# The last quarter of the last unit: activation and product in two halves, written to the buffer of an x

## The chip, the cores and the metric

The kernel runs on one core of a Trainium2 chip. The metric is the device time of one execution in microseconds (us). The engines are named as in the profile: PE (TensorE, products of matrices), PEld (its weight loads), DVE (VectorE), ACT (ScalarE), POOL (GpSimd), and SP (SyncE), which only issues transfers. ACT and POOL issue transfers too. Each engine works through its own queue in order; semaphores tie the queues together.

## What is computed

An input `x` of 16 batches, 256 rows and 256 columns, in float32, goes through two mixtures of experts, each added to its input. In the first, one expert of eight is chosen for each batch, with biases and a hidden width of 512. In the second, two experts of eight are chosen and weighted, and a shared expert is added for every batch, with a hidden width of 1024.

```python
# first layer, for each batch, with its expert's weights
x = x + (silu(x @ wu.T + bu) * (x @ wg.T + bg)) @ wd.T + bd
# second layer: two chosen experts, weighted, and the shared one
mlp = lambda g, u, d: (gelu(x @ g) * (x @ u)) @ d
x = x + w1 * mlp(*expert1) + w2 * mlp(*expert2) + mlp(*shared)
```

## The kernel before

Everything is kept transposed, features on the partitions and the 256 rows of a batch along the free dimension. The work is cut into units. A `Pair` is one expert with two batches; a `Single` has one batch. A pair's products are done in Strassen's way: the two batches and the two halves of a matrix make a 2 by 2 block product, which takes seven products (steps) in place of eight and some sums of blocks.

A pair of the second layer goes through four *quarters*, each a quarter of the hidden width. A quarter has seven *up* steps (`up`, L541): step by step they fill PSUM banks named X, Y and Q. ACT copies each X bank to SBUF (`copy`, L522), and DVE combines such a copy with a Y or Q bank (`combine`, L526) into one of four blocks of the tile `c`: C11, C21, C12, C22. The blocks are complete after different steps: C11 after step 1, C22 after step 4, C21 after step 5, C12 after step 6. C11 and C21 belong to the first batch of the pair, C12 and C22 to the second. When all are there, `act` applies the activation to the gate half of `c` (ACT, L577) and multiplies it by the other half (DVE, L580) into a tile of the ring `bt`; `act_sums` then adds up the blocks that the next product needs (`sums_b`, L472 to L474).

After the four quarters follow seven *down* steps (`down`, L597), each with eight matmul pieces over the four quarters' `bt` tiles, into banks A, B and Y. After a step whose bank is complete for the first time, `early` moves the bank to a small tile `dz` (ACT, L619; in the last unit DVE, L612, which adds what already stands in the output). When the second part is there, `late` adds it and writes a block of the result `ys` (L630). The first down step reads only block C11 of each quarter's activations, the second only C21, and the others read sums too.

The units overlap. The down steps of one unit are put among the up steps of the next. The order is made when the kernel is built: `Line` keeps a clock in units of PE work, `main` emits a piece and moves the clock, and `later` puts a piece at a due time, so that the order in each engine's queue is that of the due times. Buffers come from rings. Some rings, `bt` with seven tiles among them, are *held*: a tile goes back by `give`. If none is free when a piece is due, `when_free` keeps the piece until a `give` emits it. The ring `xt`, with two tiles as wide as those of `bt`, is not held and is used in turn; it holds the `x` of a unit and of the next.

The last two units are pairs of the shared expert, `shared[-2]` and `shared[-1]`. For the last one, the activation of its fourth quarter is due when all seven `bt` tiles are out: four belong to `shared[-2]`, three to its own earlier quarters. It is therefore emitted by the first `give` at the end of `shared[-2]`'s seventh down step, after that step's late sum on DVE:

```python
elif k == 6:
    late(C12, "Q", -1)
    give("d", self)
    for j in range(self.kp):
        give("bt", (self, j))
```

The results of a unit are added to the output in memory by accumulating transfers on POOL's queue (`send`, L451), one for each batch; for `shared[-2]` they are issued at once after its last down step. Each is given the rows of its batch by an index that is loaded at run time, and waits for the one before. The last unit does without: it loads what stands in the output into `z` beforehand (L515), adds it in `early`, and stores plainly, block by block, the first batch on SP's queue and the second on ACT's (L633). The first of these stores on each queue waits until POOL's transfers have landed; SP's second store also waits until SP's first has landed. After its last store each engine branches to a common end block (L1096 in the profile), where SP waits for all transfers and the engines meet.

Which experts fall in pairs is known only at run time; the program holds an arm for each case, and every arm ends with the same two shared units.

Of the kernel before, what the change touches and what calls it, by code (L numbers as in the profile page):

```python
# [10 lines left out]
AF = mybir.ActivationFunctionType  # L11
ALU = mybir.AluOpType
# [3 lines left out]
B, S, D, E = 16, 256, 256, 8  # L16
# [39 lines left out]
UP, SINGLE_UP = 2, 8  # L56
# [3 lines left out]
def kernel(  # L60
# [10 lines left out]
    nc = tc.nc  # L71
# [40 lines left out]
    def take(tag, *shape, of=None):  # L112

        i = turns[tag].pop(0)
        if tag not in HELD:
            turns[tag].append(i)
        else:
            assert (tag, of) not in turns
            turns[tag, of] = i
        t = rings[tag][i]  # L120
        n = 1
        for d in shape:
            n *= d
        t = t[:, :n]
        if len(shape) == 1:
            return t
        names = "abcd"[: len(shape)]
        return t.rearrange(
            f"p ({' '.join(names)}) -> p {' '.join(names)}", **dict(zip(names, shape))
        )  # L130

    def when_free(tag, f):

        if turns[tag] and not turns["later", tag]:
            f()
        else:
            turns["later", tag].append(f)

    def give(tag, of):
        turns[tag].append(turns.pop((tag, of)))  # L140
        if turns["later", tag]:
            turns["later", tag].pop(0)()

    def bank(tag):
        return take(tag, N2)
# [312 lines left out]
    class Pair(Unit):  # L458
# [114 lines left out]
        def act(self, j):  # L573
# [6 lines left out]
            nc.vector.tensor_tensor(t[:, 0:4, :], u, v, ALU.mult)  # L580
            self.acts.append(t)

        def act_sums(self, j):
            t = self.acts[j]
            self.sums_b(t, t[:, 2, :])

        def down(self, k):

            tag, a, b = STEPS[k]
            if k == 0:  # L590
                self.ys = take("ys", KD, 2, S, of=self)
            if OPENS[k]:
                self.banks[tag] = bank({"X": "A", "Q": "B", "Y": "Y"}[tag])
            src = self.d[:, A_AT[a]] if a in A_AT else self.ds[:, S_AT[a]]
            d = self.banks[tag][:, :S]
            for j in range(self.kp):
                nc.tensor.matmul(  # L597
                    d,
                    lhsT=src[:, j, :],
                    rhs=self.acts[j][:, B_AT[b], :],  # L600
                    start=OPENS[k] and j == 0,
                    stop=j == self.kp - 1,
                    skip_group_check=True,
                )

            def early(block):
                c, t = block % 2, block // 2
                e = take("dz", S, of=(self, block))
                self.copies[block] = e
                src = self.banks["X"][:, :S]  # L610
                if self.last:
                    nc.vector.tensor_tensor(e, self.z[:, c, t, :], src, ALU.add)  # L612
                elif not self.layer:
                    nc.vector.scalar_tensor_tensor(  # L614
                        e, src, self.bd[:, c : c + 1], self.xt[:, block, :], ALU.add, ALU.add
                    )
                else:
                    w = 1.0 if self.at is None else self.weight(t)
                    nc.scalar.activation(e, src, AF.Copy, scale=w)  # L619

            def late(block, tag, sign):
                c, t = block % 2, block // 2
                e, src = self.copies[block], self.banks[tag][:, :S]
                dst = self.ys[:, c, t, :]
                if self.layer and self.at is not None:
                    nc.vector.scalar_tensor_tensor(  # L626
                        dst, src, self.weight(t, sign), e, ALU.mult, ALU.add
                    )
                else:
                    nc.vector.tensor_tensor(dst, e, src, ALU.add if sign > 0 else ALU.subtract)  # L630
                if self.last:
                    queue = (nc.sync, nc.scalar)[t]
                    store = queue.dma_start(self.out[t][:, c, :], dst)  # L633
                    for other in self.stores[1 - t]:
                        tc.declare_no_dep(store.ins, other.ins, reason="another batch")
                    self.stores[t].append(store)
                give("dz", (self, block))

            if k == 0:
                early(C11)  # L640
            elif k == 1:
                late(C11, "Y", 1)
            elif k == 2:
                early(C12)
            elif k == 4:
                early(C22)
                early(C21)
                late(C22, "Q", -1)
            elif k == 5:
                late(C21, "Y", 1)  # L650
            elif k == 6:
                late(C12, "Q", -1)
                give("d", self)
                for j in range(self.kp):
                    give("bt", (self, j))
                if not self.layer:
                    give("bt", self)
                if not self.last:
                    self.done(self.ys)

        def run(self, line, among):

            self.start()
            for j in range(self.kp):
                line.quarter(self, j)
                for k in range(6):
                    line.main(UP, lambda j=j, k=k: self.up(j, k))

                line.later(2 * UP, lambda j=j: self.up(j, 6))
                if not self.layer:  # L670
                    line.later(UP + 1, lambda j=j: self.act0(j, 1))
                line.later(
                    3 * UP, lambda j=j: when_free("bt", lambda: self.act(j))
                )
                line.later(6 * UP, lambda j=j: self.act_sums(j))
                for f in among[j] if j < len(among) else ():
                    f()
            step = self.step or (6 if self.layer else 3)
            for k in range(7):
                line.later(self.first + step * k, lambda k=k: self.down(k))  # L680
# [262 lines left out]
    line = Line()  # L943
# [55 lines left out]
    def follow(units, behind=True):  # L999
# [3 lines left out]
        if known == start + Q_AHEAD - 1:  # L1003
            u, j = quarters[known]
            u.load_q(j, behind=behind)

    run(units[0])
    for k in arms(0):

# [10 lines left out]
        for a, p in zip(places[4:], pieces):  # L1020
            a.append(p)
        follow([*mid, *units[1], *tails[1]], behind=False)
        run([*mid, *units[1]])
        while line.routed < len(steps):
            line.route()
        for k in arms(1):
            left = ones[2 * k :]
            rest = [*tails[1], *left[:-1], *more_pairs[:k], *shared[1 - NB :]]
            turns["xs"], turns["d"] = [0, 1], [*turns["d"], 2]
            for u in rest:  # L1030
                among[u] = [[] for _ in range(u.kp)]
            if left:

                host = rest[len(left)]
                for j in range(host.kp):
                    among[host][j].append(partial(left[-1].piece, line, j, among=True))
                left[-1].po_bank, left[0].po_bank = "A", "B"
                shared[-NB].first = 24
            follow(rest)
            run(rest)  # L1040
            line.flush(1 << 30)
            line.send()
# [58 lines left out]
```

## Time and profile before

| | us |
|---|---|
| median of 3 runs | 1051.06 (1050.55 to 1051.47) |
| profiled execution | 1051.36 |
| its span | 1049.7 |
| PE busy | 1038.2 (99% of the span) |
| DVE busy | 777.0 (74%) |
| ACT busy | 371.3 (35%) |
| POOL busy | 446.7 (43%) |
| TensorE's granted clock | 0.999 |

The span is the time from the first to the last instruction of the profiled execution, which itself took 1.66 us more. Busy times overlap. Matmuls are pipelined and their ends are modelled, so that a matmul's reported duration overlaps the next. A time such as 1033.98 is counted from the start of the span. A wait for several semaphores is put down to the one that came last, which is not always the one that mattered.

### The profile page before, as it was taken

What the parts mean: (1) busy time and instruction counts of PE and PEld (TensorE: products, weight loads), DVE (VectorE), ACT (ScalarE), POOL (GpSimd) and SP (SyncE); (2) the same over time, 40 slices, a digit from 0 to 9 for tenths busy, and PEclk for the clock granted to TensorE, in tenths of its full rate; (3) what the DMA queues carried; (4) which work ended last, traced back from release to release, by engine and by line L of the source; (5) the groups of instructions that cost most, each with busy time, mean ns of one, the idle gap of its engine ahead of it and who ended that gap; (6) DMA issues with size and microseconds to landing.
All of it is one profiled execution on the core that took longest, in us unless ns stands there. A gap on an engine that the chain in (4) does not pass through costs nothing.

```text
span 1049.7 us, 14152 instructions
## 1 busy us (share of the span) xinstructions
PE 1038.2 (99%) x4750; PEld 900.3 (86%) x4750; DVE 777.0 (74%) x1207; ACT 371.3 (35%) x583; POOL 446.7 (43%) x492
## 2 busy tenths in 40 slices
PE   9999999999999999999999999999999999999998
PEld 6778888888888888888888888888888888888886
DVE  7789978878687877887777778777766236776764
ACT  2444353535333333333333333333333123333331
POOL 2946331221043765666476556645201245630000
PEclk9999999999999999999999999999999999999999
DMA  7636656656664355345335533543655445356522
GB/s 237 241 127 203 240 181 194 207 166 236 200 235 119 88 140 140 93 109 140 98 87 138 140 98 103 140 122 83 178 159 171 133 136 156 91 180 184 183 75 45
DMA packets 60974, 157.47 MB, mean 150 GB/s; under 512 B 7506, under 2 KB 27090, under 8 KB 56658
## 3 DMA queue, kind: packets, MB, share of 16 engines
q1 hardware_dynamic: 47618, 140.90, 40.3%
q0 software_dynamic: 12976, 15.21, 9.4%
q8 instruction: 42, 0.69, 0.3%
q14 instruction: 50, 0.41, 0.1%
q10 hardware_dynamic: 288, 0.26, 0.1%
HBM read 132.23 MB, written 24.12 MB: 149 GB/s over the span
## 4 chain that ended last, share of the span: by engine, by line
PE 89%; DVE 7%; issue 2%; ACT 1%; DMA 1%; SPq 0%; DVEq 0%; ACTq 0%
PE X L541 24%; PE Q L541 16%; PE Y L541 16%; PE A L597 12%; PE B L597 9%; PE Y L597 8%; DVE c L526 2%; PE X L692 2%; PE Q L692 1%; DVE bt L580 1%; PE A L722 1%; DVE bt L472 1%; DVE bt L473 1%; PE B L722 1%; ACT c L577 1%
## 5 line engine op out<-in xcount | busy, mean ns | idle before, releaser
L522 ACT ACTIVATE cp<-X 128x512 f32<-128x512 f32 x318 | 189.5, 596 | 519.2 <-PE X L541 518.6
L580 DVE TENSOR_TENSOR bt<-c 128x1024 f32<-128x1024 f32 x106 | 145.7, 1374 | 102.8 <-ACT c L577 93.0
L541 PE MATMUL Y<-xt,q 128*128 128x256 f32 x736 | 189.8, 380 | 1.1 <-DVE c L526 0.6
L541 PE MATMUL Q<-xt,s 128*128 128x256 f32 x736 | 189.5, 380 | 0.6 <-DVE c L526 0.6
L541 PE MATMUL X<-xt,s 128*128 128x256 f32 x736 | 189.5, 380 | 0.0
L526 DVE TENSOR_TENSOR c<-cp,Q 128x512 f32<-128x512 f32 x212 | 144.3, 681 | 37.4 <-ACT cp L522 32.9
L526 DVE TENSOR_TENSOR c<-cp,Y 128x512 f32<-128x512 f32 x212 | 144.1, 680 | 22.4 <-PE Y L541 22.0
L541 PEld LDWEIGHTS Y<-xt,q 128*128 128x128 f32 x736 | 138.9, 190 | 23.2 <-DVE c L526 3.9
L451 POOL DMA_DIRECT2D out_dram<-ys x46 | 49.0, 1065 | 255.7 <-DVE ys L626 103.2
L541 PEld LDWEIGHTS Q<-xt,s 128*128 128x128 f32 x736 | 139.3, 190 | 21.2 <-DVE c L526 2.5
L541 PEld LDWEIGHTS X<-xt,s 128*128 128x128 f32 x736 | 139.3, 190 | 20.5 <-ACT cp L522 1.4
L479 POOL TENSOR_TENSOR s<-q 128x256 f32<-128x256 f32 x78 | 72.1, 924 | 131.8 <-PE Q L541 66.2
L482 POOL TENSOR_TENSOR s<-s,q 128x256 f32<-128x256 f32 x78 | 62.5, 801 | 101.0 <-PE Q L541 101.0
L597 PE MATMUL A<-bt,ds 128*128 128x256 f32 x424 | 101.5, 379 | 1.4 <-DVE dz L614 1.4
L597 PE MATMUL B<-bt,ds 128*128 128x256 f32 x424 | 101.4, 379 | 0.0
L577 ACT ACTIVATE c<-c 128x1024 f32<-128x1024 f32 x92 | 96.7, 1052 | 12.9 <-DVE c L526 12.7
L472 DVE TENSOR_TENSOR bt<-bt 128x512 f32<-128x512 f32 x113 | 95.0, 840 | 0.7 <-DMA bt<-x_dram 0.6
L541 PE MATMUL X<-xt,q 128*128 128x256 f32 x368 | 94.4, 379 | 0.0
L597 PEld LDWEIGHTS A<-bt,ds 128*128 128x128 f32 x424 | 80.4, 190 | 13.0 <-POOL s L481 1.4
L597 PEld LDWEIGHTS B<-bt,ds 128*128 128x128 f32 x424 | 80.5, 190 | 11.2 <-ACT ys L737 0.3
L597 PE MATMUL Y<-bt,d 128*128 128x256 f32 x376 | 90.0, 379 | 0.0
L597 PEld LDWEIGHTS Y<-bt,d 128*128 128x128 f32 x376 | 71.4, 190 | 9.7
(163 smaller groups left out, 1157.1 us busy)
## 6 DMA issues: line engine op xcount, KB each, us to landing
q<-wq_dram SPq DMA_DIRECT2D x114, 512.0 KB, 3.7
d<-wd_dram SPq DMA_DIRECT2D x22, 1024.0 KB, 6.6
s<-qsums SPq DMA_DIRECT2D x28, 512.0 KB, 4.9
xt<-x1d SPq DMA_DIRECT2D x46, 256.0 KB, 4.3
out_dram<-ys POOLq DMA_DIRECT2D x46, 256.0 KB, 5.1
ds<-dsums SPq DMA_DIRECT2D x7, 1024.0 KB, 6.3
d<-wd_dram SPq DMA_DIRECT2D x7, 513.0 KB, 5.1
bt<-x_dram SPq DMA_DIRECT2D x14, 256.0 KB, 4.7
```

The costliest lines, as they stand in the source:

```text
L451: nc.gpsimd.dma_start(row(out), ys[:, :, t, :], accum_op=ALU.add)
L472: tt(t[:, 4:6, :], t[:, 0:3:2, :], t[:, 2:4, :], ALU.subtract)
L479: tt(s("S1"), a("A21"), a("A22"), ALU.add)
L482: tt(s("nS4"), s("S2"), a("A12"), ALU.subtract)
L522: nc.scalar.activation(t, self.banks["X", j], AF.Copy)
L526: nc.vector.tensor_tensor(self.c[j][:, block].rearrange("p m s -> p (m s)"), self.copies[n, j], self.banks[tag, j], op,)
L541: nc.tensor.matmul(self.banks[tag, j][:, bass.ts(m, S)], lhsT=self.q[j][:, m, A_AT[a], :] if a in A_AT else self.s[j][:, m, S_AT[a], :], r ...
L577: nc.scalar.activation(u, u, AF.Gelu_apprx_tanh)
L580: nc.vector.tensor_tensor(t[:, 0:4, :], u, v, ALU.mult)
L597: nc.tensor.matmul(d, lhsT=src[:, j, :], rhs=self.acts[j][:, B_AT[b], :], start=OPENS[k] and j == 0, stop=j == self.kp - 1, skip_group_che ...
L692: nc.tensor.matmul(dst[:, bass.ts(half, S)], lhsT=self.q[j][:, m, 2 * half + c, :], rhs=self.xt[:, c, :], start=(c == 0), stop=(c == KD - 1),)
L722: nc.tensor.matmul(self.po[:, bass.ts(c, S)], lhsT=self.d[:, 2 * c + half, j, :], rhs=self.acts[j][:, bass.ts(half, S)], start=(j == 0 and ...
```

## The change

In the last unit's fourth quarter, activation and product are done in two halves by batch. The first half (C11 and C21) is due one clock unit after the quarter's sixth up step is emitted, the second (C12 and C22) right after the seventh. The product is written to a tile of `xt`, so nothing has to be given back first; the pieces are no longer passed through `when_free`. The unit then gives back three `bt` tiles in place of four.

```diff
+        def act_half(self, j, half):
+
+            if half == 0:
+
+                self.acts.append(take("xt", 7, S))
+            t, k = self.acts[j], slice(2 * half, 2 * half + 2)
+            u, v = self.c[j][:, k, 0, :], self.c[j][:, k, 1, :]
+            nc.scalar.activation(u, u, AF.Gelu_apprx_tanh)
+            nc.vector.tensor_tensor(t[:, k, :], u, v, ALU.mult)
+
...
-                for j in range(self.kp):
+                for j in range(self.kp - self.last):
                     give("bt", (self, j))
...
-                line.later(
-                    3 * UP, lambda j=j: when_free("bt", lambda: self.act(j))
-                )
+                if self.last and j == self.kp - 1:
+
+                    line.later(1, lambda: self.act_half(j, 0))
+                    line.later(2 * UP, lambda: self.act_half(j, 1))
+                else:
+                    line.later(3 * UP, lambda j=j: when_free("bt", lambda: self.act(j)))
```

On each engine's queue in the arm that runs, this changes the end as follows. ACT has two activations of half the size in place of one, still ahead of its stores. DVE has this order:

```
before: sums of quarter 2 (L472 to L474), combine C12, late C21 and late C12 of
        shared[-2], product, sums of quarter 3, first early sum of the last unit
after:  sums of quarter 2, product half 0, combine C12, product half 1, late C21
        and late C12 of shared[-2], sums of quarter 3, first early sum
```

The orders on PE, POOL and SP stay as they were.

## The prediction

> **What bounds the kernel now.** I read the page first. Its busy row says that TensorE (PE) works without a break at full clock, so a gain can only come from a place where PE waits, or from the tail after its last product.
>
> ```profile
> span 1049.7 us, 14152 instructions
> ...
> PE 1038.2 (99%) x4750; PEld 900.3 (86%) x4750; DVE 777.0 (74%) x1207; ACT 371.3 (35%) x583; POOL 446.7 (43%) x492
> ```
>
> Next, PE's own waits over the whole span: the only one on a line that this change touches is 0.4 us behind the product of L580.
>
> ```profile
> PE A L597 <- DVE bt L580: 0.4, 1, 0.4
> ```
>
> The timeline shows where it stands: at 1033.98, in the last unit's first down step. Columns are start, duration, engine and line, with idle time in brackets.
>
> ```profile
> 1030.18 0.68 DVE L526 TENSOR_TENSOR c<-cp,Q 128x512 f32<-128x512 f32 x1
> ...
> 1030.78 0.42 DVE L630 TENSOR_TENSOR ys<-dz,Y 128x256 f32<-128x256 f32 x1
> 1030.95 1.06 ACT L577 ACTIVATE c<-c 128x1024 f32<-128x1024 f32 x1 [3.11 <-DVE c L526]
> 1031.49 1.08 POOL L451 DMA_DIRECT2D out_dram<-ys  x1 [31.09 <-DVE ys L630]
> ...
> 1032.37 0.42 DVE L630 TENSOR_TENSOR ys<-dz,B 128x256 f32<-128x256 f32 x1 [1.18 <-PE B L597]
> 1032.70 1.22 DVE L580 TENSOR_TENSOR bt<-c 128x1024 f32<-128x1024 f32 x1
> ...
> 1033.98 0.70 PE L597 MATMUL A<-bt,spare 128*128 128x256 f32 x2 [0.35 <-DVE bt L580]
> ...
> 1036.19 1.07 POOL L451 DMA_DIRECT2D out_dram<-ys  x1 [3.63 <-DVE dz L612]
> ```
>
> The activation was done at 1032.0, but its product stood on DVE behind the late sum of 1032.37, which waited for bank B. The bracket (0.35) understates the loss. In the chain of work that ended last, the step before ends at 1032.34; eight matmul pieces take 1.73 there, so the next step could begin at 1034.07. It begins at 1034.67:
>
> ```profile
> 1030.60 1.74 PE B L597 x8
> ...
> 1033.98 0.70 PE A L597 x2
> 1034.67 1.73 PE Y L597 x8
> ```
>
> PE loses **0.60 us**, and that is all the change can free.
>
> Last, the tail. PE's last sum is read at 1045.07; the final stores and the end of the program follow.
>
> ```profile
> 1040.94 3.19 SPq L633 DMA_DIRECT2D out_dram<-ys  x2
> ...
> 1042.74 3.13 ACTq L633 DMA_DIRECT2D out_dram<-ys  x2
> ```
>
> By the rows of L633, SP's two stores start at 1040.9 and 1043.8, ACT's at 1042.7 and 1045.5. SP's first could have gone at 1036.86, when its data was ready, but waits for the previous unit's two accumulating stores on POOL. Those are serial: the first starts at 1031.49 and lands after 4.1, at 1035.6, where POOL's last wait on L451 ends; the second starts at 1036.19 (the releaser that the timeline names, L612, only came last by chance), lands after 4.2, at 1040.4, and SP goes at 1040.94. SP's second store then waits for its own first (landed after 2.2, at 1043.16) and for data at 1043.77.
>
> [...] in the rows of the end block (first and last start):
>
> ```profile
> L1096 SPq EVENT_SEMAPHORE  x14: 17/28/28, 1046.9 to 1049.6; - x14
> ...
> L1096 SPq COMPARE_BRANCH  x2: 54/56/58, 1044.2 to 1044.7; - x2
> ...
> L1096 ACTq COMPARE_BRANCH  x2: 43/46/50, 1045.9 to 1046.3; - x2
> ...
> L1096 ACTq DRAIN  x2: 8/44/81, 1048.8 to 1049.1; - x2
> ```
>
> SP branches at 1044.7 and runs on at 1046.9, ACT at 1046.3 and 1048.8: 2.2 and 2.5 us that start only after each engine's last store. [...] the store at 994.1, with DVE busy throughout, lands after 4.3. What lengthens these stores in the trace is other traffic: the one at 957.9, beside 1.1 MB of loads, took 6.8.
>
> **The change, part by part.**
>
> *Moved.* The last activation and product leave the place behind the previous unit's last down step. [...] PE's, POOL's and SP's orders are unchanged, no DMA is added or moved past another, and ACT gains one instruction ahead of its final stores.
>
> *Price of the halves.* A product of 128x512 is not in the trace; the nearest row, L472 at 1033.96 (same size, two SBUF inputs), took 0.69. [...] Activation of 512: the copy of that size took 0.60[...]. I take 0.69 and 0.60; bounds 0.6 and 0.8. The pair costs DVE 0.16 more than one 1.22. The x buffer costs nothing: its last readers, the previous unit's up steps, ended four quarters earlier.
>
> *DVE worked out.* In this stretch an instruction that depends on nothing new starts 0.08 before its predecessor's reported end, a dependent one 0.03 after, and ACT 0.09 after DVE. C21's combine ends at 1028.74, so activation half 0 runs 1028.83 to 1029.43, hidden by the sums. Product half 0: 1030.18 (where C12 stood) to 1030.87. C12: 1030.79 to 1031.47. Activation half 1: 1031.56 to 1032.16. Product half 1: 1032.19 to 1032.88; DVE waits 0.7 for it. Queued behind it: late C21, 1032.80 to 1033.22 (before: 1030.78 to 1031.20); late C12 to 1033.55; the three sums to 1035.07; the first early sum 1035.00 to 1035.41 (before: to 1035.90).
>
> *PE.* It wants its first step's last pieces at 1033.64, when product half 0, the only one that step reads, has been there for 2.8 us: the stall of 0.60 goes. Next late would be the third step, which reuses bank A after the early sum: its first load moves from 1036.02 to 1035.42 against a sum ending at 1035.41, 0 to 0.05 lost. PE gains **0.57**; ACT's last store moves from 1045.53 to 1044.96.
>
> *The new wait.* Late C21 is the last input of POOL's first store and ends **2.0** later. Nothing hides that: POOL goes at 1033.49, lands 1037.6; the second goes 0.6 later, at 1038.2, and lands 1042.4; SP's first store 1042.94, landing 1045.16. SP's second, 0.53 after that landing, goes at 1045.7 instead of 1043.8. Its slack before was only 0.1: without the wait for data it would have gone at 1043.69.
>
> *The end.* SP's first wait of the end block came 3.1 after its last store, so now at 1048.8. Twelve waits at 0.06 and a drain follow: SP is done at about 1049.6 (before: 1048.4, itself waiting for ACT's last landing at 1047.96). Before, ACT was last, done at 1048.89; ACT would now be done at 1048.3. The end moves from 1048.89 to about 1049.6: **+0.7**. Bounds: if SP's first store lands with the bulk of its packets, 0.4 sooner, +0.3; if its second takes 3.9, as before, it lands at 1049.6 where SP wants it at 1049.1, +1.2.
>
> **Sum against its own time.** The profiled execution took 1051.36: span 1049.7 and 1.66 around it, 0.3 above the median of 1051.06. It would become 1052.1; the median, **1051.8**.
>
> **The rivals.**
> - *The stores have room* (late C21 is not held up, or POOL's stores land sooner). Then ACT still ends the kernel and all of PE's gain shows: 1051.06 - 0.57 = 1050.5. For it: PE leads the chain that ended last until 1045.05. Against: SP's slack of 0.1 against a delay of 2.0. Chance 0.13.
> - *Slower beyond doubt*: the shifted POOL stores take 5.8 each, as the one at 999.3 did, instead of 4.1 and 4.2. Each us passes through to SP: +3.3 on top of +0.7 gives 1055.1. It passes 0.2% once the two together are 1.4 us longer. For it: most such stores in the trace are that slow. Against: no weight loads remain at 1033 to 1042. Chance 0.06.
> - *It doesn't do what it says*: PE waits for both halves after all. Half 1 is there at 1032.88, still before 1033.64; same time as the forecast, 1051.8. Chance 0.02.
> - [...]
>
> The forecast itself has the remaining 0.79. The range runs from the full gain less some placement, 1050.0, to the forecast's upper bound plus placement, 1053.2. A measurement of this kernel can tell about 0.2%, 2.1 us, from no change; neither the forecast nor the first rival reaches that. Only the slow stores, or something that the trace does not show, do: slower 0.07, faster 0.03, no difference 0.90.
>
> **What would show it.** Right: no PE wait on the product in the last unit; two activations and two products of half size, the first product ahead of C12's combine; the late C21 sum about 2 us later, ending near 1033.2; POOL's last stores near 1033.5 and 1038.2; SP's second store near 1045.7, after ACT's last; the end block's first SP wait near 1048.8. Wrong: POOL's first store at 1031.5 as before, or SP's last store still ahead of ACT's (the gain then shows), or landings on POOL well above 4.2.

## The result and the profile after

The changed kernel takes **1053.84 us** (median of 9 runs, 1053.51 to 1055.40), the kernel before 1051.06 on the same chip (9 runs, 1049.94 to 1051.72). The ratio is 1.0031, 95% interval 1.0022 to 1.0040: slower, by 2.8 us. The forecast was 1051.8, in a range from 1050.0 to 1053.2, with a change too small to tell as the likeliest outcome. The kernel came out slower than all of that.

The profiled execution took 1053.84, with this span and these busy times:

```profile
span 1052.1 us, 14153 instructions
...
PE 1037.9 (99%) x4750; PEld 900.5 (86%) x4750; DVE 774.5 (74%) x1208; ACT 371.4 (35%) x584; POOL 446.4 (42%) x492
```

PE did the same work; what grew by 2.4 is the span. Up to the change everything lies 0.34 earlier than in the execution before (PE's B step ends at 1032.00 instead of 1032.34), so relative to that the end came 2.7 later. The line numbers have moved with the change: L590 and L591 are the new activation and product (`act_half`), L607 the down step (before L597), L640 the late sums (L630), L622 the early sum (L612), L643 the final stores (L633), L1109 the end block (L1096).

The timeline around the change (start, duration, engine, line; idle time in brackets):

```profile
1028.50 0.63 ACT L590 ACTIVATE c<-c 128x512 f32<-128x512 f32 x1 [0.99 <-DVE c L526]
...
1029.85 0.68 DVE L591 TENSOR_TENSOR xt<-c 128x512 f32<-128x512 f32 x1
...
1030.45 0.68 DVE L526 TENSOR_TENSOR c<-cp,Q 128x512 f32<-128x512 f32 x1
1031.17 0.63 ACT L590 ACTIVATE c<-c 128x512 f32<-128x512 f32 x1 [2.03 <-DVE c L526]
1031.83 0.69 DVE L591 TENSOR_TENSOR xt<-c 128x512 f32<-128x512 f32 x1 [0.70 <-ACT c L590]
...
1032.44 0.41 DVE L640 TENSOR_TENSOR ys<-dz,Y 128x256 f32<-128x256 f32 x1
...
1033.15 1.08 POOL L451 DMA_DIRECT2D out_dram<-ys  x1 [33.38 <-DVE ys L640]
...
1038.25 1.07 POOL L451 DMA_DIRECT2D out_dram<-ys  x1 [4.03 <-DMA out_dram<-ys]
```

The order on DVE is the one foretold: half 0, the combine of C12, 0.70 of waiting, half 1, and only then the late C21 sum, which ends at 1032.85 (before: 1031.20). POOL's store, which needs it, starts at 1033.15 instead of 1031.49. In the chain of work that ended last, PE no longer waits:

```profile
1030.28 1.73 PE B L607 x8
1032.00 1.73 PE A L607 x8
1033.73 1.73 PE Y L607 x8
...
1042.36 1.74 PE B L607 x8
1044.10 0.02 issue
1044.13 0.42 DVE ys L640
```

Each step begins where the one before ends. PE's last sum is read at 1044.13, 0.94 earlier than before, of which 0.34 is the head start: the change did free its **0.60**. Yet the kernel ends later. The rows of the final stores and of the end block (row: count: duration in ns, first and last start) say on which engine:

```profile
L643 ACTq DMA_DIRECT2D out_dram<-ys x2: 391/708/1026, 1043.1 to 1044.6; - x2
L643 SPq DMA_DIRECT2D out_dram<-ys x2: 338/358/377, 1043.4 to 1047.2; - x2
```

```profile
L1109 SPq EVENT_SEMAPHORE  x14: 17/28/28, 1050.5 to 1052.0; - x14
...
L1109 PEldq COMPARE_BRANCH  x2: 317/2584/4850, 1041.8 to 1042.2; - x2
...
L1109 ACTq DRAIN  x2: 8/44/81, 1048.5 to 1051.5; - x2
```

ACT's last store came 0.9 earlier than before (1044.6 for 1045.5), and its drain at 1048.5. SP's stores stand at 1043.4 and **1047.2**, where before they stood at 1040.9 and 1043.8; SP's first wait of the end block, 1046.9 before, is at 1050.5, and everyone waits for SP. The gap between SP's two stores, 2.9 before, is 3.7: the second waits for the first to land, and that took 3.6 instead of 2.2. What was on the DMA engines meanwhile (queue: packets, MB, share; then the stores of the window, with the time to landing; window 1042.6 to 1045.5):

```profile
q8 instruction: 2, 0.03, 8.1%
...
out_dram<-ys SPq DMA_DIRECT2D x1, 128.0 KB, 3.6
```

Queue q8 fetches instructions: two packets of 16 KB, from 1042.9 on, 0.7 after PE's second branch (1042.2) to the end block. In the execution before they came at 1043.8, when SP's first store (1040.9 to 1043.2) had landed, and at the same time as SP's second (1043.8). That one took 3.9 (before, same window):

```profile
q8 instruction: 2, 0.03, 7.6%
...
out_dram<-ys SPq DMA_DIRECT2D x1, 128.0 KB, 3.9
```

So the fetch met a store before as well, but the last on its queue, which no other store waits for.

### The profile page after: what moved, and what is told of

Its sections match the earlier page's. It is cut to its first block, busy times and chain, and to the rows that moved or that the text cites. A ratio compares the mean times of both kernels' runs of the same rounds, so it can differ in the third digit from the quotient of the medians.

```text
span 1052.1 us, 14153 instructions
## 1 busy us (share of the span) xinstructions
PE 1037.9 (99%) x4750; PEld 900.5 (86%) x4750; DVE 774.5 (74%) x1208; ACT 371.4 (35%) x584; POOL 446.4 (42%) x492
## 4 chain that ended last, share of the span: by engine, by line
PE 88%; DVE 5%; POOL 2%; issue 2%; DMA 1%; ACT 1%; SPq 0%; POOLq 0%; ACTq 0%; DVEq 0%
PE X L541 23%; PE Q L541 16%; PE Y L541 16%; PE A L607 12%; PE B L607 9%; PE Y L607 8%; DVE c L526 2%; PE Q L705 1%; PE X L705 1%; DVE bt L472 1%; POOL s L479 1%; PE B L735 1%; PE A L735 1%; DVE bt L580 1%; ACT c L577 1%
## 5 line engine op out<-in xcount | busy, mean ns | idle before, releaser
L607 PE MATMUL A<-bt,ds 128*128 128x256 f32 x420 | 100.6, 379 | 1.5 <-DVE dz L624 1.5
L607 PE MATMUL B<-bt,ds 128*128 128x256 f32 x420 | 100.5, 379 | 0.0
L607 PEld LDWEIGHTS A<-bt,ds 128*128 128x128 f32 x420 | 79.6, 190 | 13.0 <-POOL s L481 1.4
L607 PE MATMUL Y<-bt,d 128*128 128x256 f32 x376 | 90.0, 379 | 0.0
L607 PEld LDWEIGHTS B<-bt,ds 128*128 128x128 f32 x420 | 79.7, 190 | 11.1 <-ACT ys L750 0.3
L607 PEld LDWEIGHTS Y<-bt,d 128*128 128x128 f32 x376 | 71.4, 190 | 9.7
```

What stands on the lines that cost most here:

```text
L607: nc.tensor.matmul(d, lhsT=src[:, j, :], rhs=self.acts[j][:, B_AT[b], :], start=OPENS[k] and j == 0, stop=j == self.kp - 1, skip_group_che ...
```

## The experiments

My theory after the result had two parts. First, the late C21 sum behind the second half delays POOL's two stores and SP's two, as forecast. Second, this moves SP's first store into PE's instruction fetch, which holds up its last packets. The rivals: the halves themselves or the new buffer cost the time, by where instructions come to lie or by a wait that I had overlooked; or any later end of PE would save as much. Each ratio below is to the kernel before, run beside the experiment, with its 95% interval.

**The buffer alone.** Activation and product stay whole and stay where they were; only the tile is an `xt`.

```diff
+        def act_whole(self, j):
+            t = take("xt", 7, S)
+            u, v = self.c[j][:, :, 0, :], self.c[j][:, :, 1, :]
+            nc.scalar.activation(u, u, AF.Gelu_apprx_tanh)
+            nc.vector.tensor_tensor(t[:, 0:4, :], u, v, ALU.mult)
+            self.acts.append(t)
...
-                    line.later(1, lambda: self.act_half(j, 0))
-                    line.later(2 * UP, lambda: self.act_half(j, 1))
+                    line.later(3 * UP, lambda j=j: self.act_whole(j))
```

> The buffer alone: the last quarter's activation and product stay whole, but go to an x buffer and are due after the late C21 sum of the unit before (one activation, one product, no halves). Theory (the late C21 sum's place on DVE decides, through POOL's two serial stores and SP's two): the sum stays where it was before the change, so POOL's first late store starts within 0.3 us of its old place, SP's second store does not come after ACT's second, the product ends about 0.4 us ahead of PE's need, so PE's wait of 0.6 us is gone: 1050.5 us, against 1051.1 before and 1053.8 after. Rival (another buffer and other code places cost the time, whatever the order): about 1053.8.

Measured: 1050.47, ratio 0.9993 (0.9986 to 0.9999). Its timeline:

```profile
1030.82 0.41 DVE L647 TENSOR_TENSOR ys<-dz,Y 128x256 f32<-128x256 f32 x1
...
1032.09 1.22 DVE L597 TENSOR_TENSOR xt<-c 128x1024 f32<-128x1024 f32 x1 [0.85 <-ACT c L596]
```

The C21 sum (L647) is ahead of the product, both of SP's stores are early (1041.2 and 1043.4), and the new buffer costs nothing. It is the fastest version of all that ran, if only by 0.7 us.

**The whole product, early.** The same with due time `2 * UP`: no halves, but the product goes ahead of the late C21 sum.

> As the buffer alone, but the whole activation and product are due two clock units earlier, so that on DVE the product stands ahead of the late C21 sum: the delay without the halves. Theory (the sum's place decides): the sum waits for activation and product, some 2.4 us later than before the change, 0.4 later than with halves; PE's wait is gone all the same: 1053.5 to 1054.5 us. Rival (the halves themselves, with one more instruction each on ACT and DVE, cost the time): no halves here, so 1050.5 to 1051.1.

Measured: 1053.88, ratio 1.0027 (1.0016 to 1.0039), as slow as the change. Its timeline, and its row of the final stores:

```profile
1031.22 1.22 DVE L597 TENSOR_TENSOR xt<-c 128x1024 f32<-128x1024 f32 x1 [1.18 <-ACT c L596]
...
1032.36 0.41 DVE L647 TENSOR_TENSOR ys<-dz,Y 128x256 f32<-128x256 f32 x1
```

```profile
L650 SPq DMA_DIRECT2D out_dram<-ys x2: 338/358/378, 1042.7 to 1047.3; - x2
```

The halves aren't needed for the loss; the order on DVE is enough.

**The second half one clock unit later.** The change, with half 1 behind the late C21 sum.

```diff
-                    line.later(2 * UP, lambda: self.act_half(j, 1))
+                    line.later(2 * UP + 1, lambda: self.act_half(j, 1))
```

> The change, with its second half due one clock unit later, so that the late C21 sum stands ahead of the second product on DVE; both halves and the x buffer stay. Theory: the sum comes only 0.6 us later than before the change (behind the first product), SP's first store near 1041.5 in the time of the trace of before, its second near 1044.3, and ACT ends the kernel: 1050.6 us; if SP's first store already meets the transfers that slow it in the changed kernel, up to 1052.7. Rival (halves or code places): 1053.8.

Measured: 1051.08, ratio 1.0002 (0.9993 to 1.0010). The timeline:

```profile
1031.16 0.42 DVE L640 TENSOR_TENSOR ys<-dz,Y 128x256 f32<-128x256 f32 x1
...
1031.93 0.69 DVE L591 TENSOR_TENSOR xt<-c 128x512 f32<-128x512 f32 x1 [0.36 <-ACT c L590]
```

The C21 sum starts 1.3 earlier than with the change, SP's stores stand at 1041.4 and 1043.6, and the loss is gone. These three runs settle which part of the edit costs: putting half 1 ahead of that sum.

**The halves alone.** Halves in a `bt` tile, in the old place, through `when_free`.

```diff
+        def act_halves(self, j):
+            t = take("bt", 7, S, of=(self, j))
+            for half in range(2):
+                k = slice(2 * half, 2 * half + 2)
...
```

> The halves alone: activation and product in two halves by batch, but in a bt tile and in the old place, after the late C21 and C12 sums. Theory (PE's first down step needs only the first half, done about 0.2 us ahead of need; the sums stay in place): PE's wait is gone and the time is that of the buffer alone, 1050.5 us. Rival (one more instruction on ACT and DVE in every arm, or the halves, cost the time): about 1053.8.

Measured: 1051.47, ratio 1.0008 (0.9999 to 1.0016). That is 1.0 over what was expected, and no gain over the kernel before (1050.69 beside it), but far from 1053.8. PE has one wait there that the change has not, 0.2 behind the early sum for bank A. I can't tell this version from the kernel before, and why it isn't as fast as the buffer alone stays open.

**Block C21's final store on POOL's queue.** To take away SP's second wait, the store of C21 moves from SP to POOL, first in the change, then in the buffer alone.

```diff
...
-                    queue = (nc.sync, nc.scalar)[t]
-                    store = queue.dma_start(self.out[t][:, c, :], dst)
+                    q = 2 if block == C21 else t
+                    queue = (nc.sync, nc.scalar, nc.gpsimd)[q]
+                    store = queue.dma_start(self.out[q][:, c, :], dst)
...
```

> The change, with one store moved: block C21 of the last unit goes out on POOL's queue in place of SP's, so that it no longer waits for the landing of SP's first store. The late C21 sum and POOL's accumulating stores stay as late as in the changed kernel. Theory (the end hangs on SP's second store behind the landing of its first): SP is in the end block by about 1046.6 in the time of the changed trace, POOL's store starts near 1042.9 and lands by 1047.5, and ACT ends the kernel: 2.5 to 2.8 us less, about 1051.1. Rival (DVE's, PE's or the code's part in the change costs the time, SP's second store is only late and not the cause): about 1053.8.

> The buffer alone (whole activation and product in an x buffer, after the late C21 sum), and block C21's store on POOL's queue. Theory (in the buffer alone ACT's last store and its branch already end the kernel): no gain over the buffer alone, 1050.5 us. Rival (SP's second store still sets part of the end there): up to 0.5 us less, 1050.0.

Measured: 1052.58, ratio 1.0018 (1.0010 to 1.0026), and 1052.48, ratio 1.0016 (1.0010 to 1.0023): both missed, by 1.5 and 2.0. The rows of the end block, of the change with this store and then of the buffer alone with it:

```profile
L1111 POOLq DRAIN  x3: 44/109/3310, 1046.8 to 1050.6; - x3
L1111 SPq DRAIN  x3: 7/7/13, 1048.1 to 1050.4; - x3
```

```profile
L1117 POOLq DRAIN  x3: 44/109/3310, 1047.6 to 1051.4; - x3
...
L1117 ACTq DRAIN  x2: 8/44/81, 1048.7 to 1051.2; - x2
```

In the change with this store SP is done at 1048.1, where it had been the last at 1051.2, but a new wait takes its place: POOL's drain, which follows its own last store, takes 3.3, to 1050.1 and 1050.9, and now ends the kernel. In the buffer alone, which had nothing to save, the third queue cost 2.4 us (1.0016 against 0.9993 above). The two are level once SP's pair of stores is broken up, which fits the theory, but as POOL ends both it doesn't prove it.

**PE kept busy at its end.** Six more matmuls, whose result nobody reads, behind PE's last step, to put off its fetch.

```diff
...
+            for _ in range(6):
+                nc.tensor.matmul(
+                    t[:, :S], lhsT=self.ds[:, 0, 0, :], rhs=self.acts[0][:, 0, :], start=True, stop=True
+                )
...
```

> The change, with six more matmuls of 128x256 at PE's end, into a bank that nobody reads any more: 2.6 us more of PE work ahead of its branch to the end block. In the changed kernel SP's first store lands after 3.6 us in place of 2.2, and SP's second waits for it. Theory (the two long fetches of instructions, 16 KB each, that follow PE's branch hold up the last packets of that store): the fetches come 2.6 us later, SP's first store lands after about 2.2, SP's second starts 1.3 sooner, and the kernel is faster with more work: about 1052.5 us. Rival (SP's and ACT's first stores start within 0.3 us and slow each other): 1053.8, unchanged. Second rival (PE's end sets the time): 1056.

Measured: 1054.34, ratio 1.0026 (1.0014 to 1.0037): missed. The row of PE's branches says why:

```profile
L1118 PEldq COMPARE_BRANCH  x2: 3813/3863/3913, 1043.0 to 1047.1; - x2
```

PE's queue reached its first branch at 1043.0, with the matmuls still to run (the last ends at 1047); a fetch of one packet came at 1044.0, in the middle of SP's store (1043.0, landed after 3.8). The experiment didn't do what it was meant to, and says nothing against the theory.

**PE held back.** The change, and then an instruction that PE has to wait for: behind the last sum DVE copies the idle bank Q, and one matmul writes that bank. Nobody reads either result.

```diff
+        def hold_pe(self):
+            t, u = self.banks["Q", self.kp - 1], take("cp", N2, of="hold")
+            nc.vector.tensor_copy(u, t)
+            nc.tensor.matmul(
+                t[:, :S], lhsT=self.ds[:, 0, 0, :], rhs=self.acts[0][:, 0, :], start=True, stop=True
+            )
...
```

> The change, with PE held back from the end block: one DVE copy of an idle bank after DVE's last sum, and one matmul of 128x256 into that bank, which must wait for the copy. PE's branch then comes near 1045.3 in place of 1042.2 in the time of the changed trace. Theory (the two fetches of 16 KB that follow PE's branch hold up the last packets of SP's first store): that store lands in about 2.2 us in place of 3.6, SP's second starts 1.3 sooner, and the kernel ends about 1.3 sooner in spite of the added work: 1052.5 us. Rival (SP's and ACT's first stores slow each other, 0.3 us apart): unchanged, 1053.8. Second rival (PE's later arrival at the end block sets the end): 1054.5 or more.

Measured: 1051.75, ratio 1.0012 (1.0004 to 1.0020). With more work than the change the kernel is about 2 us faster. PE's branches stand at 1046.0 and 1046.4, and in the transfers from 1042.6 to 1045.5 there is no q8:

```profile
q10 hardware_dynamic: 144, 0.13, 13.8%
q1 hardware_dynamic: 144, 0.13, 13.5%
q14 instruction: 1, 0.01, 1.2%
q0 software_dynamic: 2, 0.00, 0.1%
...
out_dram<-ys SPq DMA_DIRECT2D x1, 128.0 KB, 2.2
```

```profile
L643 SPq DMA_DIRECT2D out_dram<-ys x2: 338/360/382, 1043.6 to 1046.0; - x2
```

SP's first store is as late as with the change, but it lands after 2.2, and the second goes at 1046.0 instead of 1047.2. The fetch has moved with PE's branch, to 1047.1, so it is PE's. And the rival that SP's and ACT's first stores slow each other fails: they start 0.3 apart here too (1043.3 and 1043.6). The profiled execution took 1052.88, 1.1 more than the median: one of the slower ones of this kernel.

**The buffer alone, with PE held back.** If holding PE saved time anywhere, it would here too.

> The buffer alone, with PE held back from the end block as in the run that held it in the change (one DVE copy, one matmul that waits for it). Theory: in the buffer alone SP's first store has landed before the fetches of instructions start, so holding PE takes nothing away from that wait; ACT's last store and branch set the end, and PE gets to the end block about 0.5 us later than ACT at most: 1050.5 us, as without the hold, up to 1051.5 if PE's arrival then sets the end. Rival (holding PE saves time in any kernel, for a reason other than SP's first store): 1.0 to 1.7 us less than the buffer alone, 1049.0.

Measured: 1052.08, ratio 1.0011 (1.0005 to 1.0018), where the buffer alone had 0.9993. Here the hold costs 1.9: SP's stores are as early as without it (1041.1 and 1043.4), and PE's own drain, at 1049.3, is the last. SP's second store lands after 1.7, where in the buffer alone, with the fetch on it, it took 4.5; but no store waits for that one. So holding PE helped where the fetch lay on SP's first store, and not where it didn't.

**The change again**, beside the last one.

> The change itself once more, on the chip of the buffer alone with PE held, to stand beside it and beside the held change: 1.0027 to 1.0035 of the kernel before, about 2.8 us more. If the held change's gain was a matter of the chip, this run comes out near 1.0012.

Measured: 1053.66, ratio 1.0032 (1.0021 to 1.0043). SP's stores:

```profile
L643 SPq DMA_DIRECT2D out_dram<-ys x2: 338/360/382, 1041.8 to 1046.4; - x2
```

In this execution POOL's stores landed after 4.1 and 4.2, and everything up to them lies 0.9 earlier than in the first profile of the change, so SP's first store went at 1041.8; but the fetch came at 1042.0, and the store landed only after 4.5.

Over all twelve profiles, the start of SP's first store, the first q8 packet of PE's fetch, and the store's time to landing:

| kernel | store | fetch | landing |
|---|---|---|---|
| halves alone | 1040.7 | 1042.9 | 2.0 |
| before | 1040.9 | 1043.8 | 2.2 |
| buffer alone, PE held | 1041.1 | 1046.8 | 2.2 |
| buffer alone | 1041.2 | 1043.2 | 2.0 |
| buffer alone, C21 on POOL | 1041.1 | 1043.4 | 1.7 |
| second half later | 1041.4 | 1043.2 | 2.0 |
| change, PE held | 1043.6 | 1047.1 | 2.2 |
| change | 1043.4 | 1042.9 | **3.6** |
| six more matmuls | 1043.0 | 1044.0 | **3.8** |
| change again | 1041.8 | 1042.0 | **4.5** |
| change, C21 on POOL | 1041.9 | 1042.4 | **4.5** |
| whole product, early | 1042.7 | 1042.7 | **4.5** |

Where the fetch starts 1.8 or more after the store, the landing is 1.7 to 2.2; where it starts from 0.6 before it to 1.0 after, 3.6 to 4.5. SP's second store fits in: where the first escapes, in before, the buffer alone, the second half later and the halves alone, the same fetch starts within 0.4 of the second, and that lands after 3.6 to 4.5. Of the change's first store, 126 packets of queue q1 had moved by 1045.4 and the last 18 only after 1045.8. How a fetch keeps the last packets back isn't shown.

## Why the prediction was wrong

**Right:** PE's wait and its size (0.60 freed, 0.57 forecast; no loss at bank A). The prices of the halves: 0.68 and 0.69 on DVE where 0.69 was taken, the time of a row of that size in the trace of before; 0.63 on ACT for 0.60. The order on DVE, the late C21 sum (ends 1032.85; forecast 1033.22, less the head start of 0.34), and the delay of 2.0 that it hands to POOL. That ACT's last store would come earlier and that SP would take its place as the last: up to the landing of SP's first store the chain was there, link by link.

**Wrong: a term in "The new wait".** The prediction put "SP's first store 1042.94, landing 1045.16", and so took over the 2.2 of the execution before. It measured 3.6. The forecast did allow a slow landing of 3.9, but for SP's second store alone, where before had shown it. The first store is the one that gates: before, it had landed ahead of PE's fetch, and the change moved it 2.5 later, while the fetch came 0.9 sooner, as PE was done sooner. They met. That PE takes a branch, and fetches, ahead of SP and ACT wasn't in the working at all: only the branches of SP and ACT were read. PE's row stands among those of the same block:

```profile
L1096 PEldq COMPARE_BRANCH  x2: 317/2562/4806, 1042.8 to 1043.2; - x2
```

The 3.9 of SP's second store goes with the fetch of these branches, at 1043.8; in the buffer alone holding PE took that store from 4.5 to 1.7. The forecast's own start of SP's first store, 1042.94, lay only 0.9 ahead of that fetch, closer than the 1.0 at which the six more matmuls had a landing of 3.8.

The sum, term by term, each as measured less as forecast and with the head start taken out: POOL's two landings 4.5 and 4.7 for 4.1 and 4.2, +0.8 before rounding; SP's first landing 3.6 for 2.2, +1.4; the second store 0.1 behind that landing and not 0.5, -0.4; so SP's second store at 1047.5 for 1045.7, +1.8. SP's first wait of the end block came 3.3 after it for 3.1, +0.2. Together +2.0 on the forecast +0.7, and the end moved by 2.7.

Not all of these are the change's in every execution. The second profile of the change has POOL's landings as forecast, 4.5 for SP's first store and 3.9 from the second store to the end block's wait, and nearly the same time. The fetch on SP's first store is in both. Holding PE took about 2 us off: SP's second store then stands at 1046.0, near the forecast's 1045.7, and the kernel at 1.1 over before, near the forecast's +0.7. That nearness proves little, as the hold itself cost 1.9 in the buffer alone.

**The rivals.** "The stores have room" failed: the late C21 sum was held up by 2.0, against SP's slack of 0.1. The buffer alone, which leaves the sum in place, shows the gain that this rival hoped for. "It doesn't do what it says" made no difference, as both halves were done by 1032.52, ahead of PE's use of them at 1033.13. "Slower beyond doubt" had the right sign, and the excess of 2.0 over the forecast is past the 1.4 that it named, but by another mechanism: it priced slow landings on POOL beside loads, and only 0.8 of the 2.0 stood there. The 1 us either way that the range holds for placement was the author's guess, worked out from no number of the traces; where the fetch fell was readable, in the transfers by window.

Three readings of the trace of before were off, though no term of the sum hung on them. DVE was not busy throughout the store of 994.1, which landed after 4.3 with no other transfer beside it: it waited 1.9 for bank B, up to 998.55. In the 6.8 of the store at 957.9 SP's queue moved 1.78 MB, not 1.1; beside the store at 999.3, which took 5.8, it moved 1.05. And most of POOL's stores were not as slow as 5.8: the median of the 46 landed after 5.1.

What stays open: why POOL's stores took 0.8 longer in one execution of the change and not in the other, and which part of the 1.1 that is left with PE held is the late order and which the extra work.

## What to carry to other kernels

Where one store on a queue waits for another, the time to landing of the first is part of the chain. Here it was 2.2 us where the store stood before and 3.6 where the change moved it, beside an instruction fetch: look at the transfers of the stretch to which a change moves a store, instruction fetches included, and not at the duration in the old place. In this kernel the engine that finished early branched to the end block early (in the change PE's second branch stands at 1042.2, ACT's at 1046.1, SP's at 1048.0), and its fetch, from 1042.9 on, fell on what the others were still storing. To free an engine's wait, put the work where nothing that leads to the last store is queued behind it: here the buffer alone freed PE's wait with no loss (1050.47, ratio 0.9993, where the change had 1.0031).

## What the runs showed of the hardware

With an instruction fetch of one or two 16 KB packets that began from 0.6 us before to 1.0 after it, SP's first store of 128 KB landed after 3.6 to 4.5 instead of 1.7 to 2.2. PE's queue reached a branch well before its last matmul had run: with six more matmuls behind the last step, which ran until 1047, it branched at 1043.0; a matmul that had to wait for DVE put the branch off to 1046.0, from 1041.8 in the change. With the store of C21 on POOL's queue, POOL's drain behind it took 3.3 us and ended the kernel; in the buffer alone, where SP and ACT had been enough, this third queue cost 2.4 us.
